# A graph layer on Trainium2: two edges of one target share a partition in a pair of tiles

## The chip, the core and the metric

The kernel runs on one core of a Trainium2 chip. The metric is the device time of one execution in microseconds. The core has TensorE (PE, with its weight loads as PEld), VectorE (DVE), ScalarE (ACT), GpSimd (POOL) and SyncE (SP, which issues most transfers), and 16 DMA engines.

## The reference

A graph has N = 12500 nodes with 128 features each and E = 412500 edges, sorted by their target, among them one self loop for each node. For an edge from src to dst:

```python
theta = x[dst] - x[src]
w = sigmoid(relu(theta @ W1 + b1) @ W2 + b2)
agg = segment_sum(w * theta, dst)
indeg = segment_sum(1, dst)
out = layernorm(x + agg + indeg * (x @ W4 + b4))
```

A self loop has theta = 0. It adds nothing to agg, and 1 to indeg.

## The kernel before

**Tables.** In the first 300 to 400 us the kernel multiplies all nodes by W1 and writes rows z = [x W1 | x] (256 floats, 1 KB) to DRAM, and the target's side y = x W1 + b1 as three bf16 addends (y3d). Then an edge needs no product with W1 of its own: it takes a row z of its source and a row y of its target.

**Parts.** Edges are worked on in parts, in order of target. The first 20 ("plain") parts have 1024 edges. Each later part has CE = 1182: 1024 in slots, 8 tiles (K) of 128; 128 "hot" ones, whose source is below 2 x 1152, fetched by products with a one-hot from a table in SBUF; and self loops, which are dropped, since they need no row (their count is added back at the end). There are NS = 352 parts, the last with 778 edges and 7 tiles. Two parts (SUB) form a block; a block's targets lie in a window of WB = 96 nodes, a part's in a window of SW = 41.

**Placement.** `place()` finds the slots of 128 parts at a time, one part in each partition, in three sets (128, 128 and 76 parts). It picks the hot edges (L511, L513), then moves kept edges over the gaps. Its operations are mostly DVE's, given out in small steps between the parts. It leaves src_i (the source of each slot), rel (target less the block's base) and rows_d in DRAM (target less the part's base, with the hot edges' behind it).

**One part**, in the names that the profile shows:

- POOL gathers 8 tiles of 128 rows z by indirect DMA into zbuf (L340), one tile an instruction.
- SP broadcasts a block's rows_d to all partitions (to_all, L688), 2 x 1152 bf16. ACT makes the one-hot oh[target, slot] of it in two instructions (L772, L773).
- PE spreads the rows of the targets over the slots, ph = oh^T y, 8 products (L781, `spread_y`).
- DVE makes ow[slot, target], 128 x 8 x 96 (L791, `one_hot_w`); then ph - z (L824), relu times W2 (L825), and the sum over features (L828).
- ACT takes the sigmoid twice (L829 for the weights, L830 into wx); DVE weighs the rows into wx (L839, `weigh`). The last two of wx's 130 columns are the weight and a 1.
- The hot edges go the same way in one tile: `hot_fetch` every fourth part on DVE (L884) and PE (L891), then L904, L905, L915, L918, L920.
- PE adds up, pa += ow^T wx, 8 products of 130 float columns, two instructions each (L940), a ninth for the hot tile and one for the carry of the block before (`sh`). pa has one buffer.
- At a block's end ACT copies pa to a (L951, `total`), which is also carried into the next block. Two blocks later `normalize` (L963, L964, L970 and on) makes the output rows.

**What sets the order.** A scheduler orders each engine's instructions, apart from SP's. POOL is paced by hand: gather k of part s waits for a step of TensorE in part s - LAG (6), if that part has a step k. Such steps are the last product of `spread_y` (0 and 1), the transpose in `own_u` (2, L707), the last product of `add_up` (5) and `hot_rows` (7):

```python
if s - LAG >= NH and (s - LAG, k) in steps_of:
    waits.append((steps_of[s - LAG, k], mybir.DependencyClass.Sync))
```

Gathers are issued 4 parts ahead (AHEAD), into 9 buffers (NZ).

A column of flags in `bad` notes whether the edges fit this plan; if one is set, a general path is run afterwards.

Of the kernel before, what the change touches and what calls it, by code (L numbers as in the profile page):

```python
# [19 lines left out]
P = 128  # L20
D = 128
K = 8
BE = K * P
# [7 lines left out]
NZ = 9  # L31
AHEAD = 4
# [10 lines left out]
RW = BE + HK  # L43
# [5 lines left out]
CE = 1182  # L49
# [7 lines left out]
def gnn_resnorm(  # L57
# [45 lines left out]
    KT = -(-TAIL // P)  # L103
    assert NS == NF + 1 and NS % SUB == 0 and TAIL <= BE and SUB == 2 and N < BIG

# [36 lines left out]
    def load(i):  # L142

        s0, n, full = sets[i]
        es = ep.tile([P, CE], I32, name="es")
        ed = ep.tile([P, CE + 1], I32, name="ed")
        e0 = E1 + (s0 - PLAIN) * CE
        if full < n:
            nc.vector.memset(es[:n, :], 0)
# [69 lines left out]
    oh_buf = [const.tile([P, K + 1, P], BF16, name=f"oh{i}") for i in range(2)]  # L219
# [78 lines left out]
    wx_buf = [const.tile([P, K, AW], F32, name=f"wx{i}") for i in range(2)]  # L298
# [19 lines left out]
    def tiles(s):  # L318
        return K if s < NF else KT

# [15 lines left out]
    def gather(s):  # L336

        (src_i, _, _), i = set_of(s)
        for k in range(tiles(s)):
# [101 lines left out]
    def place(i, ps, es, ed, bb):  # L441
# [9 lines left out]
        c = ep.tile([P, 6], F32, name="col")[:n]  # L451
# [9 lines left out]
        v.tensor_scalar(b[:full, 1:2], c[:full, 3:4], -1.0, float(CE - BE - HR * HS),  # L461
                        op0=OP.mult, op1=OP.add)
# [5 lines left out]
        t = ep.tile([P, CE], F32, name="et")[:n]  # L468
        nc.scalar.activation(t, ed[:, :CE], AF.Identity, scale=float(BIG), bias=c[:, 0:1])
        C = CE // 3  # L470
        for j in range(3):
            at = slice(j * C, (j + 1) * C)
            step = ps.tile([P, G, P], F32, name=bank).rearrange("p g d -> p (g d)")[:n, :C]
            v.tensor_sub(step, ed[:, j * C + 1:(j + 1) * C + 1], ed[:, at])
            q = ep.tile([P, P * G], F32, name="eq")[:n, :C]
            v.tensor_sub(q, es[:, at], ed[:, at])
            v.tensor_mul(q, q, step)
            v.scalar_tensor_tensor(t[:, at], step, 0.0, t[:, at], op0=OP.is_equal, op1=OP.mult)
# [11 lines left out]
        key = ep.tile([P, CE + 1], F32, name="ed")[:n, :CE]  # L490
# [3 lines left out]
        for r in range(HR):  # L494
            apart = aparts[r][:n]
            whole = CE // PM * PM
# [3 lines left out]
                apart.rearrange("p (o m) -> p o m", o=1).to_broadcast([n, CE // PM, PM]), op=OP.add)  # L500
            if whole < CE:
                v.tensor_tensor(key[:, whole:], t[:, whole:], apart[:, :CE - whole], op=OP.add)
# [32 lines left out]
        nc.sync.dma_start(rows_d[:n, BE:], hd[:, 1, :])  # L535
        hots[s0] = hot_s, hrel, n

        w = ep.tile([P, CE], I32, name="ew")[:n]
        C = CE // 6
        for j in range(6):  # L540
            at = slice(j * C, (j + 1) * C)
            pw = ps.tile([P, G, P], F32, name=bank).rearrange("p g d -> p (g d)")[:n]
            count = pw[:, :C]
            q = ep.tile([P, P * G], F32, name="eq")[:n]
            keep, out_ = q[:, :C], q[:, C:2 * C]
            v.tensor_scalar(keep, t[:, at], float(NOT * BIG), None, op0=OP.is_ge)
            v.scalar_tensor_tensor(w[:, at], t[:, at], float((2 * NOT - 1) * BIG), keep,
                                   op0=OP.min, op1=OP.mult)
            v.tensor_scalar(out_, keep, -1.0, 1.0, op0=OP.mult, op1=OP.add)
            v.tensor_tensor_scan(count, out_, most[:n].to_broadcast([n, C]),  # L550
                                 c[:, 4:5] if j else 0.0, op0=OP.add, op1=OP.min)
            v.tensor_copy(c[:, 4:5], count[:, C - 1:])
            move = out_.bitcast(I32)
            far_on = pw[:, C:2 * C]
# [6 lines left out]
        v.tensor_sub(b[:full, 10:11], c[:full, 4:5], c[:full, 3:4])  # L561
        v.tensor_scalar(b[:full, 10:11], b[:full, 10:11], -float(HR * HS), None, op0=OP.add)
        v.tensor_scalar(b[:full, 11:12], b[:full, 10:11], -1.0, None, op0=OP.mult)
        assert SW + HR * HS < LAST + P
        for r, m in enumerate([1 << r for r in range(7)] + [LAST]):
            u = ep.tile([P, CE], I32, name="ew" if r % 2 else "et")[:n]
            C = bits.shape[1] - m
            for c0 in range(0, CE, C):
                c2 = min(c0 + C + m, CE)
# [9 lines left out]
                if c2 == CE:  # L579
                    break  # L580
            w = u
        to = ep.tile([P, CE + 1], I32, name="ed")[:n, :BE]
        v.tensor_scalar(to, w[:, :BE], BIG.bit_length() - 1, 2 * NOT - 1,
                        op0=OP.logical_shift_right, op1=OP.bitwise_and)
        off = ep.tile([P, P * G], F32, name="eq").bitcast(BF16)
        nc.scalar.activation(off[:n], to, AF.Identity, bias=c[:, 1:2])
        nc.sync.dma_start(rows_d[:n, :BE], off[:n])
        yield
        t = ep.tile([P, CE], F32, name="et")[:n]
        nc.scalar.activation(t[:, :BE], to, AF.Identity, bias=c[:, 2:3])  # L590
        src_i = pp.tile([P, K, P], I32, name="src_i")
        rel = pp.tile([P, K, P], BF16, name="rel")
        f = ep.tile([P, CE], F32, name="es")[:n]
# [3 lines left out]
        for e, to in ((f, src_i), (t, rel)):  # L597
            for k0 in range(0, K, G):
                pt = ps.tile([P, G, P], F32, name=bank)
                for j in range(G):  # L600
                    nc.tensor.transpose(pt[:, j, :n], e[:, (k0 + j) * P:(k0 + j + 1) * P],
                                        ident[:n, :n])
                nc.scalar.activation(to[:, k0:k0 + G, :n], pt[:, :, :n], AF.Copy)
                yield
        placed[s0] = src_i, rel, rows_d

    with tc.manual_schedule(engines={SP}), tc.tile_pool(name="work", bufs=2) as wp, tc.tile_pool(
# [142 lines left out]
        def one_hot(s, half):  # L750


            n0, n1 = half * G, min(half * G + G, tiles(s))
# [14 lines left out]
            elif half == 0:  # L768
                b, h = divmod(s, SUB)
                at = blocks[b]["to_all"].rearrange("p h (k e) -> p h k e", e=P)  # L770
                gap = oh[:3 * SW]
# [3 lines left out]
        def spread_y(s):  # L775
# [4 lines left out]
            for k in range(tiles(s) if s >= NH else 0):  # L780
                got = nc.tensor.matmul(d["ph"][:, k, :], d["oh"][:, k, :], blocks[b]["y3"][h],  # L781
                                       start=True, stop=True)
                if k == tiles(s) - 1:
                    step(s - 1, 9 * (1 - h), got)

        def one_hot_w(s):

            n = tiles(s)
            (_, rel, _), i = set_of(s)
            ow = wp.tile([P, K, WB], F32, name="ow", bufs=2)[:, :n, :]  # L790
            nc.vector.tensor_tensor(ow, iota_f.to_broadcast([P, n, WB]),  # L791
                                    rel[:, :n, i:i + 1].to_broadcast([P, n, WB]), op=OP.is_equal)
            parts[s]["ow"] = ow
# [17 lines left out]
        def weights(s):  # L811
            n = tiles(s)
            d = parts[s]
            zs = rows_of(s)
            xs = zs if s < NH else zs[:, :, D:]
            wx = wx_buf[s % 2]
            h = d["ph"]
            if s < NH:
                both(s)
                nc.vector.scalar_tensor_tensor(  # L820
                    h, d["ph"], 0.0, w2_f.to_broadcast([P, K, D]), op0=OP.max, op1=OP.mult)
            else:
                ph = d["ph"][:, :n, :]
                nc.vector.tensor_sub(ph, ph, zs[:, :n, :D])  # L824
                nc.vector.scalar_tensor_tensor(  # L825
                    h[:, :n, :], ph, 0.0, w2_f.to_broadcast([P, n, D]), op0=OP.max, op1=OP.mult)
            lg = wp.tile([P, K], F32, name="lg")
            summed = nc.vector.tensor_reduce(lg[:, :n], h[:, :n, :], AX.X, OP.add)  # L828
            nc.scalar.activation(gate[:, s % 2, :n], lg[:, :n], AF.Sigmoid, bias=b2_c)  # L829
            nc.scalar.activation(wx[:, :n, D], lg[:, :n], AF.Sigmoid, bias=b2_c)  # L830
            return summed

        def weigh(s):

            n = tiles(s)
            zs = rows_of(s)
            xs = zs if s < NH else zs[:, :, D:]
            w = gate[:, s % 2, :n].rearrange("p (k e) -> p k e", e=1)
            return nc.vector.tensor_tensor(wx_buf[s % 2][:, :n, :D], xs[:, :n, :],  # L839
                                           w.to_broadcast([P, n, D]), op=OP.mult)  # L840
# [57 lines left out]
        def hot_rows(s):  # L898
# [6 lines left out]
            got = nc.tensor.matmul(px[:, 0, :], d["oh"][:, K, :], blocks[b]["y3"][h],  # L905
# [16 lines left out]
        def add_up(s):  # L922

            n = tiles(s)
# [6 lines left out]
            terms = [(d["ow"][:, k, :], wx_buf[s % 2][:, k, :]) for k in range(n)]  # L931
# [7 lines left out]
            for i, (one, w) in enumerate(terms):  # L939
                summed = nc.tensor.matmul(pa, one, w, start=h == 0 and i == 0,  # L940
# [5 lines left out]
        def total(b):  # L946
# [4 lines left out]
            nc.scalar.activation(a[:WB], pa, AF.Copy)  # L951
# [4 lines left out]
            d.update(a=a, sw=sw[:WB, 0:1], deg=sw[:WB, 1:] if b * SUB >= PLAIN else a[:WB, D + 1:])  # L956
# [92 lines left out]
        for s in range(NS + 1):  # L1049
# [33 lines left out]
            if s + 2 < NS and tiles(s + 2) > G:  # L1083
# [14 lines left out]
        with after(weighted):  # L1098
            normalize(NK - 1)
# [200 lines left out]
```

## Time and profile before

| | us |
|---|---|
| median of 3 runs | 4624.89 |
| lowest, highest | 4624.53, 4639.22 |
| the profiled execution | 4628.1 |
| its span, first to last instruction | 4626.2 |
| PE, PEld busy | 2636.8, 1988.8 |
| DVE, ACT, POOL busy | 3121.2, 1603.8, 2681.1 |
| mean granted TensorE clock | 0.729 of full speed |
| DMA | 539.42 MB, 117 GB/s |

The profile is of one execution. L340 is line 340 of the kernel. A group's row has the line, the engine, the operation, the tiles out<-in and the count; then the busy time in us, the mean of one in ns, the idle time of the engine just before them, and what ended most of it. "issue" means that the engine waited for nothing that the profile shows; "remote" is a semaphore event that no instruction of the core is found for.

### The profile page before, as it was taken

The numbers are of one execution on the slowest core, as the hardware profiler recorded it, in microseconds if no ns is written. First come the engines' busy times: TensorE is split into PE (matmuls) and PEld (weight loads), VectorE is DVE, ScalarE is ACT, GpSimd is POOL, SyncE is SP. The second block draws the span as 40 slices with busy tenths as digits, with TensorE's granted clock in tenths as the row PEclk, the third lists the DMA queues.
The fourth block names the chain that finished last, engine by engine and source line by source line (L and its number), as shares of the span: only waits on it lengthen the run. The fifth ranks groups of instructions, "written<-read, shape, count | busy, mean of one in ns | idle before, by whom it ended". The sixth has DMA issues, their size and how long they took to land. (4 is left out here: it accounts for less than half of the span.)

```text
span 4626.2 us, 47225 instructions
## 1 busy us (share of the span) xinstructions
PE 2636.8 (57%) x14207; PEld 1988.8 (43%) x14207; DVE 3121.2 (67%) x5030; ACT 1603.8 (35%) x3344; POOL 2681.1 (58%) x2824
## 2 busy tenths in 40 slices
PE   4355556665655555655565655556555556555555
PEld 4344344444444444444444444444444444444444
DVE  5676667777776666666777776777666566566666
ACT  4233333333333333333333333333333333333333
POOL 4415656666565566665556656656656565655663
PEclk6676777767777777777777777776777777777777
DMA  6303433443443344434333433434433443333432
GB/s 247 111 28 108 126 115 114 122 121 112 118 122 110 109 125 122 120 114 122 112 118 116 121 109 115 123 111 123 121 112 112 121 120 117 116 116 114 120 113 67
DMA packets 269164, 539.42 MB, mean 117 GB/s; under 512 B 101349, under 2 KB 152737, under 8 KB 267365
## 3 DMA queue, kind: packets, MB, share of 16 engines
q0 software_dynamic: 134096, 364.95, 27.2%
q1 hardware_dynamic: 132834, 164.97, 11.2%
q10 hardware_dynamic: 1970, 6.40, 0.5%
q8 instruction: 115, 1.88, 0.2%
q14 instruction: 149, 1.21, 0.1%
HBM read 504.19 MB, written 31.90 MB: 116 GB/s over the span
## 5 line engine op out<-in xcount | busy, mean ns | idle before, releaser
L340 POOL DMA_INDIRECT zbuf<-z,src_i x2655 | 2524.2, 951 | 1645.1 <-issue 695.5
L940 PE MATMUL pa<-wx,ow 128*96 128x130 f32 x5630 | 1125.8, 374 | 847.3 <-ACT a L951 339.9
L940 PEld LDWEIGHTS pa<-wx,ow 128*96 128x96 f32 x5630 | 1006.2, 238 | 953.9 <-ACT a L951 366.8
L839 DVE TENSOR_TENSOR wx<-zbuf,fix 128x1024 f32<-128x1024 f32 x352 | 427.3, 1214 | 601.0 <-ACT fix L829 449.2
L772 ACT ACTIVATE oh<-to_all,away 123x1152 bf16<-123x1152 bf16 x332 | 415.7, 1252 | 689.8 <-remote 350.2
L891 PE MATMUL pd<-of,tabs 128*128 128x512 bf16 (+1 forms) x2322 | 543.1, 385 | 91.2 <-issue 90.7
L791 DVE TENSOR_TENSOR ow<-fix,rel 128x768 f32<-128x768 f32 x352 | 333.5, 947 | 300.3 <-remote 296.7
L884 DVE TENSOR_TENSOR of<-hot_src,fix 128x1536 bf16<-128x1536 f16 (+1 forms) x258 | 422.2, 1690 | 10.8 <-remote 8.6
L828 DVE TENSOR_REDUCE lg<-ph 128x8 f32<-128x1024 f32 x352 | 427.0, 1213 | 0.0
L824 DVE TENSOR_TENSOR ph<-ph,zbuf 128x1024 f32<-128x1024 f32 x344 | 420.2, 1222 | 8.8 <-issue 3.2
L904 PE MATMUL pw<-wni,xT 128*128 128x256 f32 x664 | 301.7, 548 | 210.1 <-ACT wxh L918 106.2
L825 DVE SCALAR_TENSOR_TENSOR ph<-ph,w_r 128x1024 f32<-128x1024 f32 x344 | 420.7, 1223 | 0.0
L891 PEld LDWEIGHTS <-tabs 128*128 128x128 bf16 x2322 | 233.1, 101 | 363.3 <-issue 150.5
L773 ACT ACTIVATE oh<-oh 123x1152 bf16<-123x1152 bf16 x332 | 384.1, 1157 | 6.4
L781 PE MATMUL ph<-y,oh 128*128 128x128 bf16 x2751 | 261.0, 244 | 180.5 <-DVE lg L828 121.3
L781 PEld LDWEIGHTS <-oh 128*128 128x128 bf16 x2751 | 215.7, 111 | 246.5 <-issue 211.5
L915 DVE SCALAR_TENSOR_TENSOR hh<-pw,w_r 128x128 f32<-128x128 f32 x332 | 92.6, 279 | 285.5 <-PE pw L905 181.2
L940 PE MATMUL pa<-a,sh 96*96 96x130 f32 x350 | 106.2, 398 | 287.7 <-issue 85.4
L963 ACT ACTIVATE pw<-xw,sw 96x128 f32<-96x128 f32 x176 | 64.6, 367 | 545.2 <-issue 241.4
L904 PEld LDWEIGHTS pw<-wni,xT 128*128 128x128 f32 x664 | 142.7, 266 | 246.4 <-ACT wxh L918 135.9
L895 ACT ACTIVATE xT<-pd 128x512 f32<-128x512 f32 (+1 forms) x86 | 50.1, 582 | 481.6 <-PE pd L891 388.4
L951 ACT ACTIVATE a<-pa 96x130 f32<-96x130 f32 x176 | 47.8, 272 | 459.4 <-remote 398.5
(257 smaller groups left out, 2925.5 us busy)
## 6 DMA issues: line engine op xcount, KB each, us to landing
to_all<-off_d SPq DMA_DIRECT2D x166, 576.0 KB
zbuf<-z,src_i POOLq DMA_INDIRECT x2655
z<-zbuf SPq DMA_DIRECT2D x12, 1024.0 KB
y<-y3d SPq DMA_DIRECT2D x342, 30.8 KB
y3d<-tabs SPq DMA_DIRECT2D x12, 768.0 KB
xw<-in_x_dram SPq DMA_DIRECT2D x176, 48.0 KB
out_dram<-o SPq DMA_DIRECT2D x176, 48.0 KB
zbuf<-in_x_dram ACTq DMA_DIRECT2D x12, 512.0 KB
```

What stands on the lines that cost most here:

```text
L340: ins = nc.gpsimd.indirect_dma_start(out=rows_of(s)[:, k, :], out_offset=None, in_=z if s >= NH else x, in_offset=IndirectOffsetOnAxis(ap= ...
L772: nc.scalar.activation(gap, at[:3 * SW, h], AF.Abs, bias=away[:3 * SW])
L773: nc.scalar.activation(gap, gap, AF.Relu, scale=-1.0, bias=1.0)
L781: got = nc.tensor.matmul(d["ph"][:, k, :], d["oh"][:, k, :], blocks[b]["y3"][h], start=True, stop=True)
L824: nc.vector.tensor_sub(ph, ph, zs[:, :n, :D])
L825: nc.vector.scalar_tensor_tensor(h[:, :n, :], ph, 0.0, w2_f.to_broadcast([P, n, D]), op0=OP.max, op1=OP.mult)
L828: summed = nc.vector.tensor_reduce(lg[:, :n], h[:, :n, :], AX.X, OP.add)
L839: return nc.vector.tensor_tensor(wx_buf[s % 2][:, :n, :D], xs[:, :n, :], w.to_broadcast([P, n, D]), op=OP.mult)
L884: nc.vector.tensor_tensor(of, hot_src[:, r, lo:hi].rearrange("p (o e) -> p o e", o=1).to_broadcast([P, T, hi - lo]), nid[:, g * T:(g + 1) ...
L891: nc.tensor.matmul(px, tabs[:, r, g * T + t, c, :], of[:, t, :], start=g == 0 and t == 0 and c == 0, stop=g == 2 and t == T - 1 and c == 2)
L904: nc.tensor.matmul(px[:, :2, :], xT, wni, start=True, stop=False)
L940: summed = nc.tensor.matmul(pa, one, w, start=h == 0 and i == 0, stop=h == 1 and i == len(terms) - 1)
```

## The change

Tile j and tile 4 + j of a part now hold, in each partition, two edges of the same target. A target with an odd number of kept edges keeps one of its self loops as well, so that its edges pair up. Kept self loops take slots, so a part has CE = 1156 edges for its 1024 slots and 128 hot ones, and there are 360 parts (the last with 136 edges and one pair of tiles).

- rows_d and to_all have 4 x 128 + 128 = 640 columns a part; oh too.
- `spread_y` has 4 products; DVE's subtraction reads each result for both halves.
- ow has 4 tiles. `add_up` has 4 products with 2 x 130 columns, one half into each half of pa. The last column of wx in the upper half is no longer a constant 1 but a flag from rel (copied by ACT in `weights`), which is 0 for a kept self loop, so that it isn't counted twice.
- `total` copies the upper half of pa by ACT; a new `finish`, given out after the next part's weights, adds the lower half by DVE, sets the carry and makes sw.
- wx has three buffers in place of two.
- `place()` finds the odd targets by one more scan in each of 8 chunks (6 before), with some seven more DVE operations a chunk.

The 20 plain parts keep their order of edges. The core of the diff:

```diff
-CE = 1182
+CE = 1156
+WE = CE + 1
...
-RW = BE + HK
+BP = J * P
+RW = BP + HK
...
-    wx_buf = [const.tile([P, K, AW], F32, name=f"wx{i}") for i in range(2)]
+    wx_buf = [const.tile([P, K, AW], F32, name=f"wx{i}") for i in range(NW)]
...
-        for k in range(tiles(s)):
+        for k in slots(s):
...
+            odd, count, far_on = pw[:, :m + 1], pw[:, C + 1:C + 1 + m], pw[:, 2 * C + 1:2 * C + 1 + m]
...
+            v.scalar_tensor_tensor(mark, t[:, at], float(BIG), keep, op0=OP.is_ge, op1=OP.add)
+            v.tensor_scalar(mark, mark, -1.0, 1.0, op0=OP.mult, op1=OP.add)
...
+            v.tensor_tensor_scan(odd[:, 1:], mark, keep, c[:, 5:6] if j else 0.0,
+                                 op0=OP.mult, op1=OP.add)
+            v.tensor_copy(c[:, 5:6], odd[:, m:])
+            v.scalar_tensor_tensor(mark, mark, 0.0, odd[:, :m], op0=OP.is_equal, op1=OP.mult,
+                                   accum_out=c[:, 6 + j:7 + j])
+            v.tensor_add(keep, keep, mark)
...
-            for k in range(tiles(s) if s >= NH else 0):
-                got = nc.tensor.matmul(d["ph"][:, k, :], d["oh"][:, k, :], blocks[b]["y3"][h],
-                                       start=True, stop=True)
+            n, k0 = (K, 0) if s < PLAIN else (pairs(s), J)
+            for k in range(n if s >= NH else 0):
+                got = nc.tensor.matmul(d["ph"][:, k0 + k, :], d["oh"][:, k, :],
+                                       blocks[b]["y3"][h], start=True, stop=True)
...
+                if s >= PLAIN:
+                    n = pairs(s)
+                    y = y[:, J:J + n, :].rearrange("p (o k) d -> p o k d", o=1)
+                    y = y.to_broadcast([P, 2, n, D])
...
+            if s >= PLAIN:
+                (_, rel, _), i = set_of(s)
+                nc.scalar.activation(wx[:, J:, D + 1:], rel[:, J:, i:i + 1], AF.Copy)
...
-                bd["pa"] = ps_l.tile([P, AW], F32, name="pa")
+                bd["pa"] = ps_l.tile([P, 2, AW], F32, name="pa")
...
+                wx = wx.rearrange("p (h k) d -> p k h d", h=2)
+                terms = [(d["ow"][0][:, k, :], wx[:, k]) for k in range(pairs(s))]
...
-            nc.scalar.activation(a[:WB], pa, AF.Copy)
+                nc.scalar.activation(a[:WB], pa[:, 1, :], AF.Copy)
+            d.update(a=a)
+
+        def finish(b):
+
+            d = blocks[b]
+            a = d["a"]
+            if b * SUB >= PLAIN:
+                nc.vector.tensor_add(a[:WB], a[:WB], d["pa"][:WB, 0, :])
             carry[0] = a
...
+            if s % SUB and b:
+                finish(b - 1)
```

More of the change, by code (lines that the diff above doesn't have):

```diff
@@ L22 @@
 K = 8
+J = K // 2
 BE = K * P
@@ L31 @@
 NZ = 9
+NW = 3
 AHEAD = 4
@@ L148, in load @@
         if full < n:
-            nc.vector.memset(es[:n, :], 0)
+            for r in range(HR):
+                nc.vector.memset(es[:n, r::HR], r * HOT)
             nc.vector.memset(ed[:n, :], N)
@@ L218, in gnn_resnorm @@
     YB = WB + 3
-    oh_buf = [const.tile([P, K + 1, P], BF16, name=f"oh{i}") for i in range(2)]
+    oh_buf = [const.tile([P, K, P], BF16, name=f"oh{i}") for i in range(2)]
     y3_buf = [const.tile([P, SUB, D], BF16, name=f"y3{i}") for i in range(4)]
@@ L316, in gnn_resnorm, with pairs, slots, filled @@
     NX = NH // 2
-    def tiles(s):
-        return K if s < NF else KT
+    def pairs(s):
+        return J if s < NF else JT
+    def slots(s):
+        return [h * J + j for h in range(2) for j in range(pairs(s))]
+    def filled(t, s):
+        if s < NF:
+            return t
+        return t.rearrange("p (h j) d -> p h j d", h=2)[:, :, :JT, :]
     def rows_of(s):
@@ L466, in place @@
         yield
-        t = ep.tile([P, CE], F32, name="et")[:n]
-        nc.scalar.activation(t, ed[:, :CE], AF.Identity, scale=float(BIG), bias=c[:, 0:1])
-        C = CE // 3
-        for j in range(3):
[L472 to L475, printed above, removed]
+        t = ep.tile([P, WE], F32, name="et")[:n]
+        nc.scalar.activation(t[:, :CE], ed[:, :CE], AF.Identity, scale=float(BIG), bias=c[:, 0:1])
+        loop = float((NOT - 1) * BIG)
+        v.tensor_scalar(t[:, CE:], t[:, CE - 1:CE], -loop, None, op0=OP.add)
+        v.tensor_scalar(es[:, CE:], ed[:, CE - 1:CE], float(N - 1), None, op0=OP.min)
+        C = -(-CE // 3)
+        for j in range(3):
+            at = slice(j * C, min(j * C + C, CE))
+            m = at.stop - at.start
+            step = ps.tile([P, G, P], F32, name=bank).rearrange("p g d -> p (g d)")[:n, :m]
+            v.tensor_sub(step, ed[:, at.start + 1:at.stop + 1], ed[:, at])
+            q = ep.tile([P, P * G], F32, name="eq")[:n, :m]
             v.tensor_sub(q, es[:, at], ed[:, at])
             v.tensor_mul(q, q, step)
-            v.scalar_tensor_tensor(t[:, at], step, 0.0, t[:, at], op0=OP.is_equal, op1=OP.mult)
+            v.scalar_tensor_tensor(t[:, at], step, -loop, t[:, at], op0=OP.mult, op1=OP.add)
             nc.scalar.activation(step, step, AF.Square, accum_out=b[:, 4 + j:5 + j])
@@ L560, in place @@
             yield
[L561 to L562 removed]
+        v.tensor_reduce(c[:, 14:15], c[:, 6:14], AX.X, OP.add)
+        v.tensor_scalar(b[:full, 1:2], c[:full, 4:5], -1.0, float(WE - BE), op0=OP.mult, op1=OP.add)
+        v.tensor_add(c[:, 14:15], c[:, 14:15], c[:, 4:5])
+        v.tensor_sub(b[:full, 10:11], c[:full, 14:15], c[:full, 3:4])
+        v.tensor_scalar(b[:full, 10:11], b[:full, 10:11], -float(HR * HS + 1), None, op0=OP.add)
         v.tensor_scalar(b[:full, 11:12], b[:full, 10:11], -1.0, None, op0=OP.mult)
@@ L565, in place @@
         for r, m in enumerate([1 << r for r in range(7)] + [LAST]):
-            u = ep.tile([P, CE], I32, name="ew" if r % 2 else "et")[:n]
+            u = ep.tile([P, WE], I32, name="ew" if r % 2 else "et")[:n]
             C = bits.shape[1] - m
-            for c0 in range(0, CE, C):
-                c2 = min(c0 + C + m, CE)
+            for c0 in range(0, WE, C):
+                c2 = min(c0 + C + m, WE)
                 c1 = c2 - m
@@ L596, in place @@
         yield
-        for e, to in ((f, src_i), (t, rel)):
-            for k0 in range(0, K, G):
+        ends = f[:, :BE].rearrange("p (e h) -> p h e", h=2)
+        for e, to in ((ends, src_i), (t[:, :BE].rearrange("p (h e) -> p h e", h=2), rel)):
+            for h in range(2):
                 pt = ps.tile([P, G, P], F32, name=bank)
[L600 to L603, printed above, removed]
+                for j in range(J):
+                    nc.tensor.transpose(pt[:, j, :n], e[:, h, j * P:(j + 1) * P], ident[:n, :n])
+                nc.scalar.activation(to[:, h * J:(h + 1) * J, :n], pt[:, :J, :n], AF.Copy)
                 yield
@@ L750, in one_hot @@
         def one_hot(s, half):
-            n0, n1 = half * G, min(half * G + G, tiles(s))
+            n0, n1 = half * G, half * G + G
             if half == 0:
@@ L779, in spread_y @@
             d["ph"] = ps_h.tile([P, K, D], F32, name="ph")
-            for k in range(tiles(s) if s >= NH else 0):
-                got = nc.tensor.matmul(d["ph"][:, k, :], d["oh"][:, k, :], blocks[b]["y3"][h],
-                                       start=True, stop=True)
-                if k == tiles(s) - 1:
+            n, k0 = (K, 0) if s < PLAIN else (pairs(s), J)
+            for k in range(n if s >= NH else 0):
+                got = nc.tensor.matmul(d["ph"][:, k0 + k, :], d["oh"][:, k, :],
+                                       blocks[b]["y3"][h], start=True, stop=True)
+                if k == n - 1:
                     step(s - 1, 9 * (1 - h), got)
         def one_hot_w(s):
-            n = tiles(s)
             (_, rel, _), i = set_of(s)
[L790 to L793, printed above, removed]
+            n = pairs(s)
+            parts[s]["ow"] = []
+            for k0 in range(0, K if s < PLAIN else J, J):
+                ow = wp.tile([P, J, WB], F32, name="ow", bufs=4)
+                nc.vector.tensor_tensor(
+                    ow[:, :n], iota_f.to_broadcast([P, n, WB]),
+                    rel[:, k0:k0 + n, i:i + 1].to_broadcast([P, n, WB]), op=OP.is_equal)
+                parts[s]["ow"].append(ow)
         def both(s):
@@ L928, in add_up @@
             if h == 0:
-                bd["pa"] = ps_l.tile([P, AW], F32, name="pa")
+                bd["pa"] = ps_l.tile([P, 2, AW], F32, name="pa")
             pa = bd["pa"][:WB]
-            terms = [(d["ow"][:, k, :], wx_buf[s % 2][:, k, :]) for k in range(n)]
+            wx = wx_buf[s % NW]
+            if s < PLAIN:
+                terms = [(d["ow"][k // J][:, k % J, :], wx[:, k, :]) for k in range(K)]
+            else:
+                wx = wx.rearrange("p (h k) d -> p k h d", h=2)
+                terms = [(d["ow"][0][:, k, :], wx[:, k]) for k in range(pairs(s))]
             if s >= PLAIN:
@@ L939, in add_up @@
             for i, (one, w) in enumerate(terms):
-                summed = nc.tensor.matmul(pa, one, w, start=h == 0 and i == 0,
+                to = pa if len(w.shape) == 3 else pa[:, 0, :]
+                summed = nc.tensor.matmul(to, one, w, start=h == 0 and i == 0,
                                           stop=h == 1 and i == len(terms) - 1)
@@ L1082, in gnn_resnorm @@
                 one_hot(s + 2, 0)
-            if s + 2 < NS and tiles(s + 2) > G:
+            if s + 2 < NS:
                 one_hot(s + 2, 1)
```

113 lines of the change are left out of this document (62 added, 51 removed).

## The prediction

> **What bounds the kernel now.** The page first: no engine is full.
>
> ```profile
> span 4626.2 us, 47225 instructions
> PE 2636.8 (57%) x14207; PEld 1988.8 (43%) x14207; DVE 3121.2 (67%) x5030; ACT 1603.8 (35%) x3344; POOL 2681.1 (58%) x2824
> ```
>
> Then the costliest groups. POOL's one kind of work is the gather, and its largest idle time is called "issue".
>
> ```profile
> L340 POOL DMA_INDIRECT zbuf<-z,src_i x2655 | 2524.2, 951 | 1645.1 <-issue 695.5
> L940 PE MATMUL pa<-wx,ow 128*96 128x130 f32 x5630 | 1125.8, 374 | 847.3 <-ACT a L951 339.9
> L839 DVE TENSOR_TENSOR wx<-zbuf,fix 128x1024 f32<-128x1024 f32 x352 | 427.3, 1214 | 601.0 <-ACT fix L829 449.2
> L772 ACT ACTIVATE oh<-to_all,away 123x1152 bf16<-123x1152 bf16 x332 | 415.7, 1252 | 689.8 <-remote 350.2
> L791 DVE TENSOR_TENSOR ow<-fix,rel 128x768 f32<-128x768 f32 x352 | 333.5, 947 | 300.3 <-remote 296.7
> L781 PE MATMUL ph<-y,oh 128*128 128x128 bf16 x2751 | 261.0, 244 | 180.5 <-DVE lg L828 121.3
> ```
>
> Next the instructions of the gather's line and POOL's waits.
>
> ```profile
> L340 POOL DMA_INDIRECT zbuf<-z,src_i x2655: 940/946/2067, 400.5 to 4568.6; - x190
> ...
> POOL zbuf L340 <- issue: 734.6, 2345, 4.4
> POOL zbuf L340 <- PE pd L707: 422.6, 72, 16.1
> POOL zbuf L340 <- remote: 312.1, 140, 3.9
> ```
>
> "Issue" is 734.6 / 2345 = 0.31 us between two gathers, so POOL can do one in 0.951 + 0.30 = 1.25 us and a part of 8 in 10.0 us. The 2655 table gathers take (4568.6 + 0.9 - 400.5) / 2655 = 1.570 us each. The other 0.32 us a gather (2.56 us a part, 850 us in all) are stops, in which POOL waits for a step of TensorE six parts back. So one part takes 12.56 us, of which 10.0 are POOL's own.
>
> How the engines share that time is seen in a stop (timeline):
>
> ```profile
> 2587.16 0.95 POOL L340 DMA_INDIRECT zbuf<-z,src_i  x1 [0.30 <-issue]
> ...
> 2591.13 0.96 DVE L791 TENSOR_TENSOR ow<-fix,rel 128x768 f32<-128x768 f32 x1 [6.89 <-remote]
> 2591.28 0.28 ACT L951 ACTIVATE a<-pa 96x130 f32<-96x130 f32 x1 [6.95 <-remote]
> ...
> 2591.51 0.94 POOL L340 DMA_INDIRECT zbuf<-z,src_i  x1 [3.40 <-remote]
> 2591.61 1.18 PE L940 MATMUL pa<-wx,ow 128*96 128x130 f32 x4 [7.01 <-ACT a L951]
> ```
>
> DVE, ACT and PE had all stood for 7 us while gathers ran on; some 3 us after the last gather's end they start together, and the gathers too. Before that the compute engines were quick: 7.36 us between two L828 (2573.39 and 2580.75). So compute works in bursts at 7 to 8 us a part, stands, and POOL alternates with it. What holds the engines in the stand, the trace does not say.
>
> Last, the busy time by stage:
>
> ```profile
> 600.00:1200.00 600.00, 367.37 (x1869) 274.25 (x1868) 446.61 (x712) 210.03 (x442) 365.91 (x380) 0.72 0.39 116
> 1300.00:1900.00 600.00, 336.90 (x1865) 249.38 (x1864) 396.17 (x638) 212.35 (x441) 364.42 (x386) 0.76 0.40 118
> 2200.00:2800.00 600.00, 356.99 (x1858) 260.64 (x1858) 443.96 (x706) 207.85 (x440) 361.77 (x376) 0.73 0.39 116
> 2900.00:3500.00 600.00, 351.75 (x1888) 260.77 (x1889) 405.26 (x646) 212.58 (x443) 364.77 (x386) 0.73 0.40 118
> 3700.00:4300.00 600.00, 343.32 (x1858) 258.61 (x1858) 373.02 (x562) 203.28 (x431) 360.89 (x382) 0.75 0.39 117
> ```
>
> (PE, PEld, DVE, ACT, POOL, then clock, DMA share, GB/s.) The first and third hold the placement of the next edges. DVE is there at 445 us against a mean of 391, or 9.4 against 8.1 us a part; gathers are 378 on average against 384.7, so a part takes 12.70 against 12.48 us. That is 0.17 us of time for each us of DVE. Among the three others more DVE goes with less time, so 0.17 is an upper value. Load on a compute engine moves the time little; the number of gathers moves it fully.
>
> **The change, part by part.** *More parts.* With 1156 edges in place of 1182, parts go from 352 to 360 and gathers from 2815 to 359 x 8 + 2 = 2874. The 59 more cost 59 x 1.570 = +93 us at the present pace; 59 x 1.25 = +74 if no stop comes with them. I take +93. [...]
>
> *ACT's one-hot.* L772 and L773 take 1252 and 1157 ns for 1152 columns; the same two for 512 columns (L766, L767) 683 and 628. In a straight line 640 columns are 797 + 734, a saving of 0.88 us a part. The new copy of 128x4 flags is bounded by L829 (128x8, 259 ns): net -0.6 us.
>
> *DVE.* L791 at half its columns: between 947 ns (768 columns) and 287 (L964, 96x128), about 0.55 us, so -0.39. The new addition per block (96x130) is 0.29, 0.15 a part. Net -0.24 us.
>
> *PE.* L781 does 4 products in place of 8, at 261.0 / 2751 = 95 ns: -0.38 us a part. The sums have 4 products of 260 columns, which stream the same columns as 8 of 130. By L940 (200 ns busy an instruction, 16 of them) they are 3.2 us now; by L904 (256 columns, 301.7 / 664 = 454 ns, 8 of them) 3.6 after; if half the weight loads free time it is 0.5 less. I take nothing.
>
> *What these are worth.* None is on POOL. If DVE's and PE's 0.62 us shorten a burst as DVE's load lengthens it, 0.62 x 0.17 x 340 parts = -36 us; with ACT's 0.6 us also -71; if the stand takes it all, nothing. I take -36. The rest is covered by the stand; without that cover rival A holds.
>
> *The broadcast* of the offsets falls from 576 to 320 KB a block (166 x 576 KB = 96 MB to 170 x 320 KB = 54 MB). Its queue holds 11.2% of the DMA engines' time, and the one near the stop above was issued (L688, 2591.52) when the stop had ended: nothing, and it is in A if I am wrong.
>
> *The end of a block.* Now ACT copies the sum (272 ns), and the next block's first product waits for that: 339.9 us over 71 waits. After, ACT copies one half and DVE adds the other, and the product waits for DVE. The addition takes 0.29 us and can stand behind one subtraction (L824, 1.22 us): 0.29 to 1.51 us a block for PE, and behind PE's product wait the hot products (L904, L905) and the next L781. As load on the burst it is 0.15 to 0.76 us a part, x 0.17 x 340 = +9 to +44; in full on the path 170 x 1.51 = +257. I take +20.
>
> *Placement* has 8 chunks of 145 columns for 6 of 197, and some 7 more DVE operations in each: 8 x 7 x 0.29 = 16 us a set, 49 us for three; x 0.17 = +8. The third weight buffer takes a wait away from L839 only when two were short: its waits are for ACT, so nothing.
>
> Sum: 4628.1 (the profiled execution; span 4626.2) + 93 - 36 + 20 + 8 = 4713. The median of the runs is 3.2 lower: **4710 us, +1.8%**.
>
> **The rivals.**
> *A: compute's relief shortens the stops.* If gathers released at a stop go with parts done in a burst, and all 1.2 us (ACT 0.6, DVE 0.24, PE 0.38) come off its 7.4, stops shrink by 17%: 0.43 us a part, -146 us. With +93 and half of the last two terms (+14) that is 4586 us. It decides from (93 + 28) / 340 = 0.36 us a part, 14% of the stops. If the stops lose a quarter (0.64 us a part, -218) it is 4514. For it: L828 at 7.36 us in a burst, ACT oh and DVE ow waiting 350 and 297 us for "remote". Against: 1.3 us of DVE a part moves 0.2.
> *B: they cancel,* stops 0.32 to 0.40 us a part shorter: 4611 to 4639.
> *C: the end of the block is on the path.* For it: PE's 339.9 us for ACT's copy is its largest named wait. Against: a stand of 7 us covers more than 1.5. In full, 4625 + 93 + 257 + 8 = 4983; at half, 4855. It decides over 0.5 us a block.
> *D: a lower clock.* The granted clock is 0.72 to 0.76 in the stages, mean 0.729. At 0.68 PE's 2637 us would be 190 longer, 0.54 us a part, x 0.17 x 340 = +31: 4740. Products leave PE and none comes. [...]
> *E: pairing fails* and the flag sends the kernel down its general path after this one; no row prices it.
>
> **How the numbers follow.** Forecast 4640 to 4785: 0.56. A 0.27, B 0.06, C 0.05, D 0.05, E 0.01. Runs of this kernel spread 0.3% (4624.53 to 4639.22), the bound of no change. Faster 0.27 (A), same 0.06 (B), slower 0.67. The range reaches down into A, to 4550, and up to 4785: forecast plus the 44 of the last term, with the 36 not earned. It leaves out C, E and the lower part of A. The likeliest case's own range is 4640 to 4785.
>
> **What would show it.** Right: 2874 gathers, of 951 ns, at 1.53 to 1.58 us each from first to last; oh rows near 0.80 and 0.73 us, ow near 0.55; DVE busy per part little changed; clock 0.70 to 0.75. Wrong towards A: gathers under 1.50 us each, a shorter wait for PE pd L741. Towards C: a long wait of PE pa for DVE's addition. A stop that is gone altogether, or a span under 4500, would overthrow the reading that POOL and the stands set the pace.

## The result, and the profile after

The changed kernel is slower: 4773.01 us (median of 4 runs, 4762.63 to 4797.21) against 4624.71 us for the kernel before beside it (median of 4). The ratio is 1.0324, with a 95% interval from 1.0278 to 1.0371. The forecast was 4710 us, in a range of 4550 to 4785. The profiled execution took 4797.2 us; it is 24 us over the median, which has to be kept in mind in what follows.

The top of the page after:

```profile
span 4795.1 us, 40670 instructions
PE 2526.1 (53%) x10431; PEld 1592.4 (33%) x10431; DVE 3117.7 (65%) x5542; ACT 1428.5 (30%) x3757; POOL 2736.0 (57%) x2883
```

There are 6555 instructions fewer, and PE, PEld and ACT have less to do although there are eight more parts. DVE has the same: 3117.7 / 360 = 8.66 us a part, against 3121.2 / 352 = 8.87. None of this shortened the span.

The groups that answer to those of before:

```profile
L355 POOL DMA_INDIRECT zbuf<-z,src_i x2714 | 2578.4, 950 | 1735.8 <-issue 770.5
L993 PE MATMUL pa<-wx,ow 128*96 128x260 f32 (+1 forms) x3034 | 1038.6, 504 | 391.3 <-DVE wx L887 267.4
L887 DVE TENSOR_TENSOR wx<-zbuf,fix 128x1024 f32<-128x1024 f32 x360 | 437.4, 1215 | 1077.3 <-ACT fix L874 838.4
L806 ACT ACTIVATE oh<-to_all,away 123x640 bf16<-123x640 bf16 x340 | 279.7, 823 | 493.9 <-PE pw L953 167.8
L816 PE MATMUL ph<-y,oh 128*128 128x128 bf16 x1453 | 170.5, 243 | 220.4 <-issue 114.5
L828 DVE TENSOR_TENSOR ow<-fix,rel 128x384 f32<-128x384 f32 x380 | 205.5, 544 | 4.4 <-remote 2.4
```

The durations came out as forecast: a gather 950 ns, the one-hot 823 ns (0.80 us forecast), ow 544 (0.55). What grew are waits: L887 waits 838.4 us for ACT's sigmoid, 449.2 before.

The gather's line, and then POOL's waits (us in total, times, longest):

```profile
L355 POOL DMA_INDIRECT zbuf<-z,src_i x2714: 940/946/2367, 421.1 to 4734.1; - x194
```

```profile
POOL zbuf L355 <- issue: 828.3, 2482, 20.2
POOL zbuf L355 <- PE pd L741: 488.1, 76, 24.9
POOL zbuf L355 <- remote: 192.5, 71, 4.1
```

2714 table gathers in 4734.1 + 0.9 - 421.1 us are 1.590 us each; it was 1.570. PE's transpose in `own_u` (L741, L707 before) is still the step that POOL waits for most, 66 us more than before.

Where the time went is seen when the n-th gather of one trace is set against the n-th of the other (all 160 gathers of the first phase counted; start times in us):

| gather | before | after | difference |
|---|---|---|---|
| 64 | 140 | 139 | -1 |
| 128 | 350 | 370 | +20 |
| 576 | 1048 | 1068 | +20 |
| 704 | 1255 | 1309 | +54 |
| 1152 | 1952 | 1991 | +39 |
| 1280 | 2153 | 2213 | +60 |
| 1600 | 2654 | 2717 | +63 |
| 1728 | 2867 | 2960 | +93 |
| 2752 | 4471 | 4547 | +75 |
| last | 4569 | 4734 | +166 |

Gather for gather the changed kernel loses nothing over most of its length, and slowly gains. It loses in steps: 22 us in parts 8 to 16, 34 in parts 72 to 88, 30 in parts 200 to 216, and 21 in parts 144 to 160 (gathers 1152 to 1280). The first three are where `place()` makes its last count (the loop of 8 chunks, L564 to L587: 222 to 293, 1133 to 1271 and 2785 to 2922 us). At the end come the 59 more gathers, 90 us.

The windows around the second of these counts, after (PE, PEld, DVE, ACT, POOL with their instructions, clock, DMA share, GB/s):

```profile
1000.00:1130.00 130.00, 71.81 (x282) 43.29 (x282) 90.44 (x147) 38.39 (x104) 77.13 (x82) 0.71 0.37 105
1130.00:1272.00 142.00, 65.39 (x259) 39.90 (x259) 108.90 (x283) 41.13 (x106) 58.14 (x62) 0.68 0.29 83
1272.00:1400.00 128.00, 65.51 (x258) 40.12 (x258) 77.36 (x126) 29.93 (x85) 84.13 (x90) 0.70 0.36 105
```

During the count POOL starts 62 gathers in 142 us, 2.29 us each; just after it 90 in 128, 1.42 each. DVE is busy for 109 of the 142 us, so it isn't full. In the same count before (6 chunks) it was 43 gathers in 76 us, 1.77 us each:

```profile
1108.00:1184.00 76.00, 43.45 (x234) 33.87 (x233) 60.17 (x127) 26.56 (x53) 41.69 (x43) 0.73 0.36 107
```

POOL's waits in the window of the count name what it waits for, after:

```profile
POOL zbuf L355 <- PE pd L741: 66.2, 4, 24.9
```

and in the window of the same count before (1108 to 1184 us):

```profile
POOL zbuf L340 <- PE pd L707: 15.8, 1, 15.8
```

The transpose writes the PSUM tile pd, which has one buffer. Each chunk of the count takes its scratch from it as well (in the first set from pw), and keeps it from L568 or L570, just ahead of its first scan, to L586, while its operations are spread between those of the parts. By the starts and ends of these lines, the eight chunks of this count hold pd for 101 us together; in the kernel before the six hold it for 27 us (L550 to L557). The timeline shows one of the four waits end:

```profile
1160.72 0.30 DVE L586 SCALAR_TENSOR_TENSOR eq<-eq,pd 128x145 int32<-128x145 f32 x1
1161.08 0.30 PE L741 MATMUL pd<-ident,xw 96*128 96x96 f32 x1 [2.79 <-DVE eq L586]
1161.65 0.94 POOL L355 DMA_INDIRECT zbuf<-z,src_i  x1 [15.93 <-PE pd L741]
```

The chunk's last reader ends, the transpose starts 0.06 us later, and then the gather that had waited 15.93 us. PE itself had stood for only 2.79 us of that, so the line shows the hold at the end of the wait, and not how much of the wait is due to it.

### The profile page after: what moved, and what is told of

The parts are those of the page before. It is cut to its first block, busy times and chain, and to the rows that moved or that the text cites. A ratio compares the mean times of both kernels' runs of the same rounds, so it can differ in the third digit from the quotient of the medians.

```text
span 4795.1 us, 40670 instructions
## 1 busy us (share of the span) xinstructions
PE 2526.1 (53%) x10431; PEld 1592.4 (33%) x10431; DVE 3117.7 (65%) x5542; ACT 1428.5 (30%) x3757; POOL 2736.0 (57%) x2883
## 3 DMA queue, kind: packets, MB, share of 16 engines
q1 hardware_dynamic: 135830, 123.35, 8.8%
## 4 chain that ended last, share of the span: by engine, by line
another core or an unknown queue 22%; PE 22%; issue 19%; DVE 10%; ACT 9%; POOL 6%; DMA 1%; SPq 0%; DVEq 0%; ACTq 0%; POOLq 0%
PE pa L993 12%; POOL zbuf L355 6%; PE pd L939 4%; PE pw L952 3%; DVE wx L887 2%; ACT oh L806 1%; DVE ph L868 1%; ACT oh L807 1%; DVE ph L867 1%; DVE lg L873 1%; PE pd L745 1%; DMA zbuf<-z,src_i 1%; PE pd L741 1%; ACT xT L943 1%
## 5 line engine op out<-in xcount | busy, mean ns | idle before, releaser
L993 PE MATMUL pa<-wx,ow 128*96 128x260 f32 (+1 forms) x3034 | 1038.6, 504 | 391.3 <-DVE wx L887 267.4
L887 DVE TENSOR_TENSOR wx<-zbuf,fix 128x1024 f32<-128x1024 f32 x360 | 437.4, 1215 | 1077.3 <-ACT fix L874 838.4
L993 PEld LDWEIGHTS pa<-wx,ow 128*96 128x96 f32 x3034 | 631.9, 226 | 687.9 <-issue 181.0
L952 PE MATMUL pw<-wni,xT 128*128 128x256 f32 x680 | 322.9, 569 | 527.4 <-ACT wxh L966 365.4
L873 DVE TENSOR_REDUCE lg<-ph 128x8 f32<-128x1024 f32 x360 | 436.1, 1211 | 0.0
L806 ACT ACTIVATE oh<-to_all,away 123x640 bf16<-123x640 bf16 x340 | 279.7, 823 | 493.9 <-PE pw L953 167.8
L879 ACT ACTIVATE wx<-rel 128x4 f32<-128x4 bf16 x340 | 71.0, 209 | 1045.7 <-remote 690.5
L952 PEld LDWEIGHTS pw<-wni,xT 128*128 128x128 f32 x680 | 148.4, 268 | 587.4 <-ACT wxh L966 408.2
L816 PE MATMUL ph<-y,oh 128*128 128x128 bf16 x1453 | 170.5, 243 | 220.4 <-issue 114.5
L807 ACT ACTIVATE oh<-oh 123x640 bf16<-123x640 bf16 x340 | 250.0, 735 | 9.0
L741 PE MATMUL pd<-ident,xw 96*128 96x96 f32 x175 | 63.7, 364 | 331.4 <-ACT xT L943 262.4
L943 ACT ACTIVATE xT<-pd 128x512 f32<-128x512 f32 (+1 forms) x88 | 51.2, 582 | 601.8 <-remote 464.7
L993 PEld LDWEIGHTS pa<-a,sh 96*96 96x96 f32 x358 | 63.5, 229 | 495.8 <-DVE sh L988 276.1
L816 PEld LDWEIGHTS <-oh 128*128 128x128 bf16 x1453 | 122.8, 111 | 282.1 <-issue 234.0
L828 DVE TENSOR_TENSOR ow<-fix,rel 128x384 f32<-128x384 f32 x380 | 205.5, 544 | 4.4 <-remote 2.4
```

What stands on the lines that cost most here:

```text
L806: nc.scalar.activation(gap, at[:3 * SW, h], AF.Abs, bias=away[:3 * SW])
L807: nc.scalar.activation(gap, gap, AF.Relu, scale=-1.0, bias=1.0)
L816: got = nc.tensor.matmul(d["ph"][:, k0 + k, :], d["oh"][:, k, :], blocks[b]["y3"][h], start=True, stop=True)
L873: summed = nc.vector.tensor_reduce(lgs.rearrange(flat), ph, AX.X, OP.add)
L887: return nc.vector.tensor_tensor(filled(wx_buf[s % NW][:, :, :D], s), xs, w.to_broadcast(list(xs.shape)), op=OP.mult)
L952: nc.tensor.matmul(px[:, :2, :], xT, wni, start=True, stop=False)
```

## The experiments

The runs fell on three chips. On one the kernel before takes 4626 us, as in the first pair; on the two others the same program takes 3722 to 3724. What differs in the traces is the stands. Between 420 and 4566 us of the first profile PE, DVE and ACT stand still together for over 2.5 us 97 times, 587 us in all. In one trace from each of the two others (two variants of the kernel before, described below: one with another part size, one with a second half of pa) that happens 24 and 20 times, 97 and 61 us in all. POOL's wait for PE's transpose, 422.6 us in the first profile, is 8.9 and 2.4 us there. So the two others are called chips without stops here. Each result is set against the runs of the kernel before on its own chip.

**The part size alone.** The kernel before with CE = 1156 (and its chunks made to fit).

```diff
-CE = 1182
+CE = 1156
```

> The kernel before with 1156 edges a part and nothing else of the change: 360 parts, 2874 gathers. Theory G (time goes with the number of gathers, 1.570 us each): 59 x 1.57 = +93, about 4715 us. Rival (eight more parts are cheap, and the loss lies in the pairs): within 30 us of 4625.

Measured 3798.20 against 3722.31, ratio 1.0201 (1.0183 to 1.0218): +75.9 us. Its gathers, in the view of their line, and POOL's two largest waits:

```profile
L340 POOL DMA_INDIRECT zbuf<-z,src_i x2714: 942/946/2151, 361.2 to 3767.2; - x194
```

```profile
POOL zbuf L340 <- issue: 764.6, 2509, 0.6
POOL zbuf L340 <- PE ph L783: 82.2, 24, 75.2
```

A table gather takes (3767.2 + 0.9 - 361.2) / 2714 = 1.255 us, POOL's own 0.95 + 0.30. The wait for PE's transpose (L709) is 8.9 us, and the one of 75.2 us for L783 falls in the first 420 us. Here POOL alone sets the time, and 59 x 1.255 = 74. Theory G holds, with the price that belongs to a chip without stops.

**The pairs alone.** The changed kernel with CE = 1182 and one pair of tiles in the last part.

```diff
-CE = 1156
+CE = 1182
```

> The changed kernel with 1182 edges a part: all of the pairing with 352 parts and 2810 gathers. Edges that find no slot are lost, the last part has one pair of tiles, and the general path is never taken. Theory G: 64 x 1.57 = 100 us less than the changed kernel, about 4670; what is left over 4625 (some +45) is placement (+80) less relief of the engines (-35). Rival (the loss lies in the pairs): about 4750.

3751.27 against 3722.31, 1.0071 (1.0054 to 1.0088): +29 us with 5 gathers fewer (-6). So about 35 us are neither gathers nor hidden, on a chip where gathers hardly stop in the steady part (POOL's wait for L741 is 22.6 us in all).

**No search for odd targets.** The operations between `keep` and `w` in the count are left out.

```diff
-            v.scalar_tensor_tensor(mark, t[:, at], float(BIG), keep, op0=OP.is_ge, op1=OP.add)
...
-            v.tensor_tensor_scan(odd[:, 1:], mark, keep, c[:, 5:6] if j else 0.0,
-                                 op0=OP.mult, op1=OP.add)
...
-            v.tensor_add(keep, keep, mark)
```

> The changed kernel without the search for odd targets in the placement (the second scan and its operations are left out, and so no self loop is kept on purpose and pairs do not match; the general path is never taken). The cumulated gather times show the loss at three places, where the last count of each set is made: some 20 + 34 + 30 us. Theory P (placement's count costs this): about 4700, 70 less than the changed kernel. Rival F (the new end of a block costs it all through): within 15 us of 4773.

3793.82 against 3722.31, 1.0186 (1.0169 to 1.0203). The numbers expected were for a chip with stops. By ratio it is at the level of the larger part count alone (1.0201): on this chip the whole rest of the change costs nothing once the search is out.

**The scratch in SBUF.** All operations stay; the scratch takes the place of the tile "ed", which is dead by then.

```diff
-            pw = ps.tile([P, G, P], F32, name=bank).rearrange("p g d -> p (g d)")[:n]
+            pw = ep.tile([P, WE], F32, name="ed")[:n]
```

> The changed kernel with the scratch of that count in SBUF (in the place of a tile that is dead by then) in place of the one PSUM tile pd, which the transpose of the block's nodes (L741, a step that gathers wait for) and the hot fetch also use. All operations stay. Theory H (a chunk of the count holds pd through its whole chain, and the transpose and the gathers wait behind it): 4690 to 4710. Rival L (the added DVE operations cost it as load): within 15 us of 4773.

3801.68 against 3722.31, 1.0209 (1.0192 to 1.0226). Again a chip without stops, and the unedited changed kernel wasn't beside it, so this alone told H from L only through the two rows above.

**The changed kernel again.**

> The changed kernel, unedited. On the chip of the first four runs the engines did not stand (no stops in the gathers, 3722 us for the kernel before, 3798 with 1156 edges a part). Where there are no stops: 59 x 1.25 = +74 for the gathers, and by the row of 1182 edges with pairs (+29 with 5 gathers fewer) some 35 more: ratio 1.029. Where there are stops, as in the first pair of profiles: ratio 1.032.

This fell on the chip with stops: 4786.63 against 4625.94, 1.0344 (1.0281 to 1.0407). It repeats the first pair, and the steps in the gather times too: 29, 30 and 28 us at the three counts, and 19 in parts 144 to 160.

**No addition at the end of a block.**

```diff
-                nc.vector.tensor_add(a[:WB], a[:WB], d["pa"][:WB, 0, :])
+                pass
```

> The changed kernel without DVE's addition at the end of a block (the lower half of each sum is left out). Rival F (the new hop from ACT through DVE to PE lies on the path): 50 us or more below the changed kernel. Otherwise within 10 us of it.

4712.61 against 4786.63 for the changed kernel beside it, 74 us less (ratio to before 1.0165, 1.0100 to 1.0230). Rival F's 50 us are passed. The gain isn't at the counts: at gather 1024 it is 6 us, at 1792 23, at 2816 65. PE's two largest waits in the changed kernel beside it,

```profile
PE pw L952 <- ACT wxh L966: 398.1, 118, 23.5
PE pa L993 <- DVE sh L988: 330.8, 55, 17.9
```

fall to 228.2 and 261.4 us without the addition, but others come up:

```profile
PE pa L993 <- issue: 323.8, 108, 13.4
PE pa L993 <- ACT a L1007: 309.4, 84, 14.0
PE pa L993 <- DVE sh L988: 261.4, 30, 18.0
PE pw L952 <- ACT wxh L966: 228.2, 55, 21.1
```

So where engines stand, this addition is dear, and PE's waits don't say by which path. The run takes away a hop and DVE's load at once: DVE is busy 3116.6 us with the addition and 3070.2 without. At the prediction's 0.17 those 46 us would be 8, so the hop is the likelier cause, but it isn't separated.

**Fewer gathers,** in both kernels: 6 of 8 from part 40 on.

```diff
-        for k in range(tiles(s)):
+        for k in range(tiles(s) if s < 40 else min(tiles(s), K - 2)):
```

> The kernel before with 6 of the 8 gathers of a part from part 40 on (the two others are left out, so a quarter of the rows is stale). It asks how near the engines are behind POOL. If compute keeps up at 8 us a part (the burst of the first profile: 7.4): 311 parts x 2 gathers x 1.25 = 778 us less where there are no stops, down to its bound of some 8 us a part, about 3100. If the engines need 9.5 us a part, as in the last parts of the first profile, about 3570.

> The changed kernel with 6 of the 8 gathers of a part from part 40 on (a quarter of the rows is stale). If the pairs relieve the bound of the engines (rival A's premise, 0.3 to 1.2 us a part): 100 to 370 us below what the same cut makes of the kernel before, less 8 parts; if DVE bounds both (its load is 0.24 us a part less): within 70 us of it.

On the chip with stops: 4030.87 (0.8672, 0.8600 to 0.8744) and 3892.29 us (0.8412, 0.8358 to 0.8467). With eight more parts the changed kernel is some 120 us faster by the ratios (139 by the medians) than the kernel before with as few gathers, which is near the lower end of what was expected if the pairs relieve the engines. So they do, as rival A had it; with all eight gathers the changed kernel is slower all the same. Neither of the two bounds expected for the kernel before was met: it came to 4031, over both, since it still stops (POOL waits 534.2 us for PE's L707).

The two runs also price a gather on this chip. 623 fewer took about 600 us off the kernel before, some 1.0 us each, and 638 fewer took 894 off the changed one, 1.4 each, and not 1.57. There the engines hold back part of what POOL saves.

**The scratch once more, and a second half of pa.** The second kernel is the one before with a pa of two halves, used by turns:

```diff
-                bd["pa"] = ps_l.tile([P, AW], F32, name="pa")
+                bd["pa"] = pa_buf[:, b % 2, :]
```

> The changed kernel with the scratch of the placement's last count in SBUF, once more, for a chip on which the gathers are stopped (before 4626, changed 4787). There the changed kernel loses 25, 28 and 25 us in the stretches where the three counts are made. Theory H (a chunk holds the one PSUM tile pd while its operations are spread over the parts, and L741 and the gathers wait for it): about 4715, the ratio to before 1.02, and no loss at those three places. Rival L (the added DVE operations are load): 4770 to 4787. Where there are no stops it repeats 1.021.

> The kernel before with two halves of one PSUM tile for the sums, taken by turns, so that a block's first product need not wait for the copy of the last block (L951, PE's 339.9 us). Leaving out the addition in the changed kernel gave 74 us. If what counts is the wait for the one buffer of sums: 40 to 100 us faster than before where gathers are stopped. If only the extra hop counts, or the copy stands in the same stretches as everything else: within 15 us. Where there are no stops: no change.

Both ran on a chip without stops: 1.0211 (1.0194 to 1.0228), and 1.0000 (0.9990 to 1.0009). The first repeats; the second says only that the wait for pa costs nothing there. It was the one try at a kernel faster than both; on a chip with stops it wasn't run.

**The scratch beside the unedited kernel.**

> The changed kernel with the scratch of the placement's last count in SBUF, again for the case that gathers are stopped on this chip: theory H about 4715 (ratio to before 1.02), rival L 4770 to 4787 (1.032). Where there are none: 1.021, and the unedited changed kernel beside it tells what the scratch is worth there.

> The changed kernel, unedited, beside it. Where gathers are stopped: 1.032 to 1.034. Where they are not: 59 x 1.25 = +74 (1.020) if everything but the gathers is hidden, 1.02 to 1.03 if the placement shows there too (theory H: more than with the scratch in SBUF; rival L: the same).

3798.07 (1.0198, 1.0180 to 1.0216) and 3829.49 us (1.0284, 1.0266 to 1.0302) against 3723.79, on a chip without stops. The same operations with another scratch are 31 us faster, all of it at the three counts: by the n-th gather 20 us in parts 8 to 16, 6 in parts 80 to 88 and 6 in parts 208 to 216. H holds there and L falls. PE's waits between 200 and 300 us, in the unedited kernel, show the hold itself (the first set's bank is pw):

```profile
PE pw L755 <- DVE eq L586: 19.2, 1, 19.2
```

L586 is the chunk's last reader of its scratch; with the scratch in SBUF this wait is gone. The second count runs from 916 to 1038 us in the unedited kernel. At its end PE's transpose waits 7.6 us for the last chunk and POOL 6.6 us for the transpose (1038 us). Between 1020 and 1100 us this kernel

```profile
1020.00:1100.00 80.00, 51.70 (x217) 31.56 (x218) 71.00 (x145) 31.61 (x85) 55.70 (x60) 0.74 0.43 124
```

starts 60 gathers, and with the scratch in SBUF

```profile
1020.00:1100.00 80.00, 53.12 (x220) 32.43 (x219) 71.59 (x124) 32.40 (x86) 60.51 (x65) 0.77 0.47 133
```

65, as many as POOL can do at 1.25 us (its count is over by then, 898 to 994 us). The operations of all three counts, L564 to L587, take DVE 111.6 us in the unedited kernel and 110.0 with the scratch in SBUF: it isn't load, and the operations are hardly quicker in SBUF.

Without stops the account closes: 59 gathers x 1.25 = 74 and 31 for the hold are 105; measured 3829.49 - 3723.79 = 105.7.

## Why the prediction was right or wrong

**The reading.** That POOL and the stands set the pace was right. Without stands POOL alone does, and the time is its number of gathers. Where there are stands, the number of gathers doesn't move the time "fully", as the prediction has it: with six gathers a part each one left out was worth 1.0 to 1.4 us, not 1.57. Nor did the engines' work move it only a little. One addition in each block was worth 74 us, and the relief by the pairs about as much or more the other way.

**More parts, +93.** On the chip with stops the 59 gathers behind the last common one took about 90 us; the part size alone wasn't run there. On the others it cost 74 to 76, the lower end given. The price hangs on the stops, as its two ends said.

**Placement, +8.** This term failed, and it alone is more than the miss of 63 us. It priced the new operations as load on DVE (49 us of it, at 0.17). Their size was right: the counts take DVE 111.5 us after (L564 to L587) and 55.2 before (L546 to L558). But the three counts cost 22 + 34 + 30 = 86 us in the first pair. The chunks aren't heavy, but each holds the only pd (or pw) from its first to its last use, and there are more operations between the two and more chunks. The working listed queues and durations, and didn't ask which buffer the new operations sit in and who else writes it; `own_u`'s transpose, POOL's largest named wait, does. That the hold is the cause is shown on the chips without stops (31 us). On the chip with stops the hold is seen at the end of four of POOL's long waits (two each in the second and third count, 10.7 to 20.3 us), but how much of the 86 us it explains is argued: the scratch in SBUF wasn't run there. PE's waits of L952 for ACT's L966 and of L741 for ACT's L943 grew as well, from 106 to 365 and from 51 to 262 us over the whole run, and nothing here says why.

**The end of a block, +20.** Mis-sized: 74 us by the run without the addition. It is neither the load's +9 to +44 nor the full +257 of rival C. The stand didn't cover it, though it is longer than the hop (6.3 us in the median of the profile after, where the addition, L1015, takes 278 ns). The sign given for rival C, a long wait of PE for DVE's addition, didn't show (42.0 us for L1015), so that sign doesn't find the cost.

**Relief, -36.** Mis-sized as well, the other way. Outside the three counts and parts 144 to 160 the first pair's gathers gained 107 - 75 = 32 us up to gather 2752. With the addition's 74 in that, relief would be some 100 us. The trace of the run without the addition, set against the first profile, agrees: outside those four stretches its gathers gain 103 us up to gather 2752. No run has the pairs' relief alone. The two errors cancelled, so the net of both (-16 forecast, -32 seen) was near.

So 90 + 86 + 21 - 32, and 3 at the end of the span, are the 169 us between the two profiled executions' spans, of which 24 are this execution's own. The 21 us in parts 144 to 160 came again in the second pair (19); there is one wait of POOL of 20.2 us, put down to "issue". What it waited for stays open.

**Luck.** That the time came within the range owes something to luck. The two errors above cancelled, and the miss of the placement's term had no place in the range. Its upper end was to be the forecast with +44 for the end of a block and without the relief's 36. With 44 in place of 20 that is 4770, and with 44 on top 4790; the 4785 given follows from neither. The run came to 4773. The sign "1.53 to 1.58 us" for a gather was missed by a little (1.590).

**The clock, rival D.** The granted clock fell from 0.729 to 0.706, and without stops from 0.783 (1156 edges) to 0.766. Products left PE, 10431 in place of 14207, and PE was busy for 53% of the span in place of 57%, and the clock fell all the same; what lowers it isn't shown here. Its mean didn't come to the rival's 0.68, and lies in the range of 0.70 to 0.75 given as a sign. Without stops it cost nothing, since the account closes without it; with stops its share wasn't separated.

**The broadcast.** 41.6 MB less on the SP's queue (164.97 to 123.35 MB, and 11.2% to 8.8% of the DMA engines' time) brought nothing that can be seen without stops, since the account closes without it; with stops it wasn't separated.

## What to carry to other kernels

Price a new step by the buffers that it holds as well as by its time: operations that are spread between others keep a single buffer for as long as the spread lasts (here pd for 101 us in one count, 27 before), and whoever else writes that buffer waits (here 19.2 us for pw at L755, on a chip without stops). Set the n-th transfer of one trace against the n-th of the other before averaging: a loss in steps points to its place at once, where a mean pace (1.590 for 1.570 us) hides it. When a queue with its own floor sets the time (here 1.25 us a gather), a change that adds to its number must first win that back somewhere on the same queue. And ask for the profile of a second chip before a price is taken from the first (here 1.570 us a gather on one, and 1.255 on another, there with 1156 edges a part).

## What was not expected of the hardware

The same program takes 4626 us on one chip and 3722 to 3724 on two others, 24% apart, with all runs of each chip close together. Durations of single instructions agree (a gather 946 ns in the median on both kinds; in the changed kernel DVE's L873 1211 ns in the mean on both). On the chip with stops PE, DVE and ACT stand together while gathers run on, 6.2 us in the median of the 97 stands of the first profile and 16.0 at most; in 80 of them POOL too begins a pause of over 2 us before the stand ends. SP's issues of L673 inside these stands take 0.70 us in the median (26 of them, one at 2584.67 us) and 0.33 outside (140 between 420 and 4566 us). The changed kernel has less work for PE, PEld and ACT, and yet its engines stand for longer: 122 times and 865 us between 420 and 4735 us, in place of 97 and 587. What holds the engines, and whether the chip itself or something else at work on it at the time sets the chips apart, was not found, and no experiment here could settle it.
